# A four-layer graph network on one core: the opening and the job order of a pair are rearranged

## The chip, the core and the metric

One of the eight cores of a Trainium2 chip runs the kernel; the time is device microseconds of that core. TensorE (PE) multiplies matrices, VectorE (DVE), ScalarE (ACT) and GpSimd (POOL) do the elementwise work, and SyncE (SP) starts most transfers. Each engine takes its own instructions strictly in the order in which they were written.

## The reference, cut to what matters

`x` has shape (32, 512, 64): 32 batch items, 512 nodes, 64 features. `adj` is a 512 x 512 graph. Four layers each do `x = x + f(relu(layernorm(x)))`:

```python
# layer 0, three times:  v = relu([v, adj @ v] @ W1.T + b1) @ W2.T + b2
# layer 1, two times:    z = relu((adj @ z) @ w[i])
# layer 2, 8 heads and one output layer, each:
s = (h @ h.T) * graph;  s = where(s == 0, -1e16, s);  out = softmax(s) @ h + b
# layer 3:  e = leaky_relu(src[:, None] + dst[None, :]) * adj;  out = softmax(e) @ h + bias
```

Nearly all the work is in layer 2: per item, nine softmaxes over 512 x 512 scores.

## The kernel before, in words

**Tiling.** Two items make a pair, and 16 pairs go through the core. A pair's *front* (layers 0 and 1 and the features of layer 2; `front`, a generator of 25 steps F0 to F24) runs beside the attention of the pair before. F0 to F2 are a layernorm, F3 turns it, F4 to F12 are the three steps of layer 0 (in turn: a product with the weights at line 329, its copy to SBUF, and lines 363 and 317, which multiply with the turned graph `AT`, with the ReLU at line 366), F13 ends layer 0 (line 370 adds the residual), F14 to F16 are a layernorm, F17 to F20 layer 1, F21 to F23 a layernorm, F24 features.

**Units.** Attention is split into *units*, one softmax over 128 x 8 x 512 scores each: `a` to `d` and `g` to `j` are the eight head units of a pair (two heads of one item in each), `f` is the output layer of the pair before (`Out`), `e` the fourth layer of the pair before that (`Last`). For a unit:

- `s0`..`s3` make its scores: for a head or `f`, eight matmuls at line 427 and four at 430 that add the mask, into two of the four score buffers (`ps_s`, in PSUM); for `e`, two ScalarE instructions (line 699);
- `r0`..`r7` multiply by the graph and take row maxima on VectorE (line 448); each odd one also issues a negation on GpSimd (455);
- `x0`..`x3` are two exponentials each on ScalarE (459);
- `nA`, `nB` take reciprocals on VectorE (469), and normalise with four instructions each on GpSimd (471);
- `t0`..`t3` transpose 32 x 32 blocks on VectorE (477).

Two units share a weighted sum, `vA`..`vD` followed by the sum's number 0 to 4: 256 matmuls (line 487; 756 for sum 2, which weighs `e` and `f`). All four transposes of both units must be done before `vA`. For a pair of head units follow `us` (four ScalarE copies, 542), `w0 y0 w1 y1` (projections on PE at 521, four activations at 532), `o`, `c` (output product at 550, VectorE copy or add at 563 and 566), and for the second sum of an item `f0` or `f1` (571) and `h0` or `h1` (593, with 16 transfers on SP's queue). `k` and `Y` make the keys of the next two units (PE at 804, two ScalarE copies at 814). `eu`, `er`, `oA`..`oC`, `oT`, `oW`, `oN` follow sum 2: eviction, residual, a layernorm, and the features of the fourth layer (651, 662, with 36 transfers). `ZQ1` issues 16 transfers with the values of a pair's second item, which sums 3 and 4 read.

**Buffers that order the work.** All matmul results but the scores share four PSUM buffers (`ps_m`, tag `mm`), taken in turn: a sum holds four, `w0`, `w1` and `k` two each, `o` one. So `k` can begin only when the activations `y0` have read the two buffers that `w0` had. The softmax tiles (`sm`) are three, so a unit's first maximum waits until the sum that read the unit three before it has ended.

**What sets the order.** `manual_schedule` keeps the instructions in the order in which Python calls them. The jobs are called by tick (ten per pair) and, within a tick, by a rank, both from the dictionary `PLACES`, one (tick offset, rank) for each job name. It holds for every pair. What falls past the last tick follows the list `TAIL`, in which `T` and `U` are the last sums of the last pair, `E` its sum 2, `e` and `q` the fourth layer of pairs 13 and 14, `p` and `r` the output layer of pairs 14 and 15, `s` the fourth layer of pair 15.

**The opening.** Before the ticks the first pair's front runs alone, with the setup jobs of `among` between its steps (weights turned, graph turned, biases, masks `NEGM`, the four `factors` on A2, grams, vectors). Six steps of the second pair's front are called in it, after its steps 6 to 11 (`HEAD = 6`). Weights and biases are loaded by ScalarE's queue (lines 130 to 140), everything else by SP's.

Of the kernel before, what the change touches and what calls it, by code (L numbers as in the profile page):

```python
# [21 lines left out]
def gnn_stack_kernel(  # L22
# [107 lines left out]
    for j, r in enumerate(R):  # L130
        for k in range(2):
            nc.scalar.dma_start(out=W1n[r, k, r], in_=W1[:, k * D : (k + 1) * D])
        nc.scalar.dma_start(out=W2n[r, r], in_=W2)
    for k, b in enumerate((b1, b2, b_out, bias3)):
        for r in R:
            nc.scalar.dma_start(out=rows[H + k : H + k + 1, r], in_=b.rearrange("(o d) -> o d", o=1))
    nc.scalar.dma_start(out=rows[0:H, :], in_=bh)
    for j in range(2):
        nc.scalar.dma_start(out=ivt[:, j, :], in_=iv)
        nc.scalar.dma_start(out=b2bc[:, 0, j, :], in_=b2.partition_broadcast(P))  # L140
# [27 lines left out]
    I2b = const.tile([P, D], BF16, name="I2b")  # L168
# [13 lines left out]
    def graph_turned():  # L182
        for s in range(NT):
            pt = mm_ps()
            for t in range(NT):
                nc.tensor.transpose(pt[:, blk(t)], A[:, t, blk(s)], ident)
            nc.scalar.copy(AT[:, s, :], pt)
# [7 lines left out]
    def weights_joined():  # L195
        pt = mm_ps()
        for k in range(2):
            nc.tensor.matmul(pt[:, blk(k)], lhsT=W2n, rhs=W1T[:, k, 0, :], start=True, stop=True)
        nc.tensor.matmul(pt[:, 2 * P : 3 * P], lhsT=b2rep, rhs=W1T[:, 1, 0, :], start=True, stop=True)
        nc.tensor.matmul(pt[:, 3 * P : 3 * P + 1], lhsT=W1T[:, 0, 0, :], rhs=b2c, start=True, stop=True)  # L200
        for k in range(2):
            nc.vector.tensor_copy(W1T[:, k, 1, :], pt[:, blk(k)])
        nc.vector.tensor_copy(ubc[:, 0, :], pt[:, 2 * P : 3 * P])
        nc.vector.tensor_tensor(b1s, pt[:, 3 * P : 3 * P + 1], b1c, ALU.add)

    def masks():
# [3 lines left out]
        nc.vector.tensor_copy(I2b, II[:, 0, :])  # L210
# [21 lines left out]
    def grams():  # L232
# [5 lines left out]
        nc.vector.tensor_copy(WT.rearrange("p h d -> p (h d)"), pt)  # L238
# [4 lines left out]
        nc.vector.tensor_copy(G.rearrange("p h d -> p (h d)"), pt)  # L243
# [552 lines left out]
    def keys(ua, ub):  # L796
# [25 lines left out]
    HEAD = 6  # L822
    among = {
        0: [weights_turned],
        1: [biases, weights_joined, graph_turned],
        7: [masks],
        8: [lambda: factors(0)],
        9: [lambda: factors(1)],
        10: [lambda: factors(2)],
        11: [lambda: factors(3)],  # L830
        14: [grams],
        15: [vectors],
    }
    for n, _ in enumerate(first):
        for fn in among.get(n, ()):
            fn()
        if 6 <= n < 6 + HEAD:
            next(second)
# [3 lines left out]
        "begina": (0, 20), "s0a": (0, 21), "s1a": (0, 27), "s2a": (0, 97), "s3a": (0, 147), "r0a": (0, 81),  # L842
        "r1a": (0, 139), "r2a": (0, 148), "r3a": (0, 163), "r4a": (0, 214), "r5a": (0, 237),
        "r6a": (0, 242), "r7a": (0, 308), "x0a": (0, 253), "x1a": (0, 293), "x2a": (0, 298), "x3a": (1, 74),
        "t0a": (1, 118), "t1a": (1, 186), "t2a": (1, 285), "t3a": (1, 284), "nAa": (0, 310),
        "nBa": (1, 145), "beginb": (-1, 295), "s0b": (-1, 296), "s1b": (-1, 309), "s2b": (0, 195),
        "s3b": (0, 108), "r0b": (0, 52), "r1b": (0, 54), "r2b": (0, 57), "r3b": (0, 155), "r4b": (0, 234),
        "r5b": (0, 281), "r6b": (0, 226), "r7b": (0, 228), "x0b": (0, 88), "x1b": (0, 255), "x2b": (0, 314),
        "x3b": (0, 252), "t0b": (1, 84), "t1b": (1, 117), "t2b": (1, 102), "t3b": (1, 172), "nAb": (0, 286),
        "nBb": (1, 6), "beginc": (-1, 223), "s0c": (-1, 241), "s1c": (-1, 224), "s2c": (0, 166),  # L850
        "s3c": (0, 170), "r0c": (0, 83), "r1c": (0, 86), "r2c": (-1, 287), "r3c": (0, 37), "r4c": (0, 194),
        "r5c": (0, 248), "r6c": (0, 180), "r7c": (0, 185), "x0c": (0, 178), "x1c": (0, 174),
        "x2c": (0, 302), "x3c": (1, 33), "t0c": (0, 236), "t1c": (0, 299), "t2c": (1, 275), "t3c": (1, 268),
        "nAc": (0, 208), "nBc": (1, 49), "begind": (-1, 273), "s0d": (-1, 274), "s1d": (0, 28),
        "s2d": (0, 136), "s3d": (0, 71), "r0d": (0, 26), "r1d": (0, 46), "r2d": (0, 59), "r3d": (0, 78),
        "r4d": (0, 153), "r5d": (0, 182), "r6d": (0, 140), "r7d": (0, 203), "x0d": (0, 60), "x1d": (0, 163),
        "x2d": (0, 209), "x3d": (0, 238), "t0d": (0, 319), "t1d": (1, 0), "t2d": (1, 29), "t3d": (1, 38),
        "nAd": (0, 262), "nBd": (0, 294), "begine": (0, 41), "s0e": (0, 42), "s1e": (0, 62),
        "s2e": (0, 159), "s3e": (0, 55), "r0e": (0, 44), "r1e": (0, 132), "r2e": (0, 112), "r3e": (0, 152),
        "r4e": (0, 211), "r5e": (0, 216), "r6e": (0, 76), "r7e": (0, 161), "x0e": (0, 204), "x1e": (0, 183),  # L860
        "x2e": (1, 1), "x3e": (0, 258), "t0e": (1, 93), "t1e": (1, 162), "t2e": (1, 212), "t3e": (1, 263),
        "nAe": (0, 246), "nBe": (1, 129), "beginf": (-1, 103), "s0f": (-1, 312), "s1f": (-1, 104),
        "s2f": (0, 87), "s3f": (0, 151), "r0f": (0, 22), "r1f": (0, 77), "r2f": (-1, 239), "r3f": (-1, 261),
        "r4f": (0, 95), "r5f": (0, 179), "r6f": (0, 167), "r7f": (0, 259), "x0f": (0, 250), "x1f": (0, 173),
        "x2f": (0, 272), "x3f": (0, 290), "t0f": (0, 315), "t1f": (1, 43), "t2f": (1, 114), "t3f": (1, 122),
        "nAf": (0, 270), "nBf": (1, 9), "beging": (-1, 256), "s0g": (-1, 257), "s1g": (-1, 277),
        "s2g": (0, 68), "s3g": (0, 2), "r0g": (-1, 297), "r1g": (-1, 301), "r2g": (-1, 307), "r3g": (0, 23),
        "r4g": (0, 169), "r5g": (0, 229), "r6g": (0, 126), "r7g": (0, 142), "x0g": (0, 15), "x1g": (0, 47),
        "x2g": (0, 255), "x3g": (0, 249), "t0g": (0, 300), "t1g": (0, 311), "t2g": (1, 63), "t3g": (1, 64),
        "nAg": (0, 232), "nBg": (0, 260), "beginh": (0, 11), "s0h": (0, 12), "s1h": (0, 39), "s2h": (0, 99),  # L870
        "s3h": (0, 113), "r0h": (0, 75), "r1h": (0, 98), "r2h": (0, 105), "r3h": (0, 115), "r4h": (0, 124),
        "r5h": (0, 164), "r6h": (0, 133), "r7h": (0, 146), "x0h": (0, 100), "x1h": (0, 131),
        "x2h": (0, 215), "x3h": (0, 184), "t0h": (0, 265), "t1h": (1, 65), "t2h": (0, 288), "t3h": (0, 306),
        "nAh": (0, 192), "nBh": (0, 230), "begini": (0, 4), "s0i": (0, 5), "s1i": (0, 8), "s2i": (0, 67),
        "s3i": (0, 106), "r0i": (0, 13), "r1i": (0, 14), "r2i": (0, 16), "r3i": (0, 53), "r4i": (0, 111),
        "r5i": (0, 121), "r6i": (0, 190), "r7i": (0, 191), "x0i": (0, 80), "x1i": (0, 119), "x2i": (0, 235),
        "x3i": (1, 40), "t0i": (1, 89), "t1i": (1, 130), "t2i": (1, 243), "t3i": (1, 271), "nAi": (0, 267),
        "nBi": (1, 90), "beginj": (-1, 221), "s0j": (-1, 222), "s1j": (-1, 289), "s2j": (0, 144),
        "s3j": (0, 120), "r0j": (-1, 279), "r1j": (0, 17), "r2j": (0, 56), "r3j": (0, 61), "r4j": (0, 171),
        "r5j": (0, 254), "r6j": (0, 210), "r7j": (0, 225), "x0j": (0, 109), "x1j": (0, 220),  # L880
        "x2j": (0, 305), "x3j": (0, 280), "t0j": (0, 313), "t1j": (1, 66), "t2j": (1, 72), "t3j": (1, 176),
        "nAj": (0, 264), "nBj": (0, 318), "vA0": (1, 177), "vB0": (1, 198), "us0": (2, 25), "w00": (2, 70),
        "y00": (2, 82), "w10": (2, 127), "y10": (2, 150), "k0": (-1, 321), "Y0": (0, 10), "vA1": (1, 149),
        "vB1": (1, 156), "us1": (1, 282), "w01": (2, 32), "y01": (2, 45), "w11": (2, 134), "y11": (2, 143),
        "k1": (-1, 128), "Y1": (-1, 141), "vA2": (1, 135), "vB2": (1, 168), "vA3": (1, 137),
        "vB3": (1, 219), "us3": (2, 24), "w03": (2, 48), "y03": (2, 94), "w13": (2, 138), "y13": (2, 181),
        "k3": (-1, 187), "Y3": (-1, 189), "vA4": (1, 213), "vB4": (1, 233), "us4": (1, 304), "w04": (2, 34),
        "y04": (2, 85), "w14": (2, 116), "y14": (2, 125), "k4": (-1, 269), "Y4": (-1, 322), "o01": (2, 196),
        "c01": (2, 205), "o03": (2, 188), "c03": (3, 92), "f0": (4, 240), "h0": (5, 51), "o11": (2, 247),
# [160 lines left out]
```

## Time and profile before

| | us |
|---|---|
| three runs, median | 2334.38 (2334.08 to 2336.33) |
| the profiled execution, its own time | 2338.17 |
| its span | 2336.3 |
| first score block of the first pair (line 427) starts at | 82.88 |
| from one pair's line 370 to the next, pairs 8 to 9 | 135.5 |
| last pair's line 370 starts at | 2019.7 |

The page gives busy time by engine and by slice of the span. A row of the timeline is: start, length, engine, line, operation, tiles, count, and in brackets how long the engine had been idle and what released it. Matmul ends are modelled, so the length of a PE row runs over the start of the next one: prices of PE work are taken from start to start. A waits row is: who waited for whom, microseconds in all, times, the longest.

### The profile page before, as it was taken

To read this page: it belongs to the slowest core of one execution; us is meant where nothing else is said; L and a number is where in the kernel's file an instruction comes from. 1 tells how busy PE (TensorE), PEld (TensorE's weight loads), DVE (VectorE), ACT (ScalarE), POOL (GpSimd) and SP (SyncE) were. 2 spreads that over 40 slices of the span, in tenths; PEclk is the share of its full clock that TensorE was granted. 3 is DMA by queue.
4 is the path that set the end of the run, shared out by engine and by line. 5 is a ranking of instruction groups with operands and counts; after the bars stand their busy time and mean duration, and the time that the engine had idled before them with its cause. 6 is when DMAs were issued, how large, how long until landed. Compare 5 with 4: busy or idle time off the path is not lost.

```text
span 2336.3 us, 78517 instructions
## 1 busy us (share of the span) xinstructions
PE 2186.7 (94%) x32683; PEld 1172.3 (50%) x32683; DVE 1857.4 (80%) x4100; ACT 1493.1 (64%) x3752; POOL 1299.6 (56%) x2175
## 2 busy tenths in 40 slices
PE   6889999999999999999999999999999999999863
PEld 3435555555555555555555555555555555555342
DVE  3558788879888888988888898888888898887653
ACT  1346557667676766767676676767666676766544
POOL 2345465656666565565656466565656556655342
PEclk9899999999999999999999999999999999999886
DMA  5001111202121120212112021211202111211112
GB/s 122 11 15 21 25 20 23 42 14 39 21 41 26 24 42 13 41 21 39 25 27 40 13 42 21 37 25 29 39 15 42 20 31 25 31 32 19 22 25 46
DMA packets 279047, 70.20 MB, mean 30 GB/s; under 512 B 275100, under 2 KB 276132, under 8 KB 278692
## 3 DMA queue, kind: packets, MB, share of 16 engines
q1 hardware_dynamic: 277888, 65.02, 16.8%
q8 instruction: 256, 4.19, 0.8%
q14 instruction: 99, 0.81, 0.1%
q10 hardware_dynamic: 804, 0.17, 0.0%
HBM read 10.49 MB, written 4.19 MB: 6 GB/s over the span
## 4 chain that ended last, share of the span: by engine, by line
PE 76%; ACT 9%; DVE 6%; POOL 2%; SPq 2%; issue 1%; DMA 1%; ACTq 0%; DVEq 0%; POOLq 0%
PE s L427 20%; PE mm L487 17%; PE mm L317 9%; ACT sm L459 6%; PE mm L550 5%; PE mm L756 5%; PE mm L521 5%; PE s L430 5%; DVE sm L477 4%; PE mm L329 3%; PE mm L804 3%; SPq L299 2%; PE mm L363 1%; DVE sm L448 1%; PE mm L593 1%
## 5 line engine op out<-in xcount | busy, mean ns | idle before, releaser
L459 ACT ACTIVATE sm<-sm,nmx 128x512 f32<-128x512 f32 x1280 | 911.0, 720 | 238.5 <-POOL nmx L455 238.2
L471 POOL TENSOR_SCALAR sm<-sm,rs 128x512 f32<-128x512 f32 x1280 | 869.8, 699 | 149.1 <-DVE rs L469 109.0
L448 DVE CUSTOM_DVE_ANT_0 sm<-s,A 128x512 f32<-128x512 f32 x1152 | 734.0, 679 | 146.3 <-PE s L430 119.8
L477 DVE STREAM_TRANSPOSE sm<-sm 128x1024 f32<-128x1024 f32 x640 | 769.4, 1224 | 39.5 <-POOL sm L471 38.4
L427 PE MATMUL s<-ZZ,Y 64*64 64x512 f32 x4096 | 572.1, 605 | 24.9 <-ACT Y L814 14.0
L487 PE MATMUL mm<-sm,vq 32*64 32x256 f32 (+1 forms) x17152 | 502.7, 380 | 26.0 <-DVE sm L477 18.3
L455 POOL TENSOR_SCALAR nmx<-mx 128x2 f32<-128x2 f32 x640 | 148.3, 235 | 600.6 <-DVE mx L448 544.7
L487 PEld LDWEIGHTS mm<-sm,vq 32*64 32x64 f32 x17152 | 401.8, 135 | 141.7 <-issue 55.9
L427 PEld LDWEIGHTS s<-ZZ,Y 64*64 64x64 f32 x4096 | 146.9, 132 | 250.2 <-issue 112.9
L430 PE MATMUL s<-NEGM,I2b 64*64 64x512 bf16 x2304 | 257.9, 378 | 0.0
L459 ACT ACTIVATION_READ_ACCUMULATOR sm<-sm,nmx 128x1 f32 x1280 | 251.2, 196 | 0.0
L542 ACT COPY us<-mm 128x256 f32<-128x256 f32 x256 | 76.2, 382 | 156.6 <-PE mm L487 156.4
L317 PE MATMUL mm<-AT,v 128*128 128x512 f32 x384 | 173.6, 595 | 0.0
L532 ACT ACTIVATE y<-mm,cols 128x512 f32<-128x512 f32 x256 | 159.2, 684 | 11.1 <-PE mm L521 11.0
L268 POOL TENSOR_TENSOR xc<-x,nmu 128x512 f32<-128x512 f32 x48 | 54.8, 1141 | 192.1 <-DVE nmu L266 192.1
L430 PEld LDWEIGHTS <-I2b 64*64 64x64 bf16 x2304 | 81.0, 107 | 159.8 <-issue 159.2
L521 PE MATMUL mm<-us,Wh 64*64 64x512 f32 x1024 | 133.9, 592 | 23.1 <-ACT us L542 23.1
L277 POOL TENSOR_TENSOR r<-ve,mhalf 128x8 f32<-128x8 f32 x64 | 110.8, 1731 | 44.9 <-DVE ve L275 41.1
L756 PE MATMUL mm<-sm,vq 32*64 32x256 f32 x3712 | 118.0, 380 | 10.2 <-DVE sm L477 8.8
L550 PE MATMUL mm<-y,Wo_sb 128*64 128x512 f32 x512 | 126.9, 605 | 0.0
L317 PE MATMUL mm<-AT,z 128*128 128x512 f32 x256 | 120.1, 613 | 2.1 <-DVE z L281 1.4
L317 PEld LDWEIGHTS mm<-AT,v 128*128 128x128 f32 x384 | 73.2, 191 | 93.3 <-issue 91.7
(134 smaller groups left out, 2002.0 us busy)
## 6 DMA issues: line engine op xcount, KB each, us to landing
vq<-z SPq DMA_DIRECT2D x512, 32.0 KB, 1.9
vq<-hn SPq DMA_DIRECT2D x512, 32.0 KB, 1.9
vq<-h3n SPq DMA_DIRECT2D x512, 32.0 KB, 1.9
A<-in_adj_dram SPq DMA_DIRECT2D x5, 1024.0 KB
xt<-in_x_dram SPq DMA_DIRECT2D x32, 128.0 KB, 2.3
out_dram<-xo SPq DMA_DIRECT2D x32, 128.0 KB, 2.9
src<-src SPq DMA_DIRECT2D x64, 1.0 KB, 1.9
Wh<-in_L_gnn_Wh_dram SPq DMA_DIRECT2D x2, 256.0 KB
```

The costliest lines, as they stand in the source:

```text
L317: nc.tensor.matmul(pe, lhsT=v[:, m].rearrange("p j d -> p (j d)"), rhs=AT[:, m, :], start=(first and m == 0), stop=(m == NT - 1),)
L427: nc.tensor.matmul(pss[half][R[ab], :], lhsT=lhsT, rhs=rhs, start=True, stop=False)
L430: nc.tensor.matmul(pss[half][R[ab], :], lhsT=I2b[R[half], :], rhs=NEGM[R[half], k, :], start=False, stop=True,)
L448: nc.vector.tensor_tensor_reduce(self.sm[:, s, :], src, graph, 1.0, -FMAX, ALU.mult, ALU.max, self.mx[:, s : s + 1])
L459: nc.scalar.activation(self.sm[:, s, :], self.sm[:, s, :], AF.Exp, bias=self.nmx[:, s : s + 1], accum_out=self.ssum[:, s : s + 1],)
L471: nc.gpsimd.tensor_scalar(self.sm[:, s, :], self.sm[:, s, :], self.rs[:, s : s + 1], 1.0, ALU.mult, ALU.mult)
L477: nc.vector.transpose(out=two, in_=two)
L487: nc.tensor.matmul(self.u[i][R[c], 0 : weights.shape[1] * 32], lhsT=values[32 * i : 32 * i + 32, jb, :], rhs=weights[32 * i : 32 * i + 32, ...
L521: nc.tensor.matmul(py[c][r, :], lhsT=Wh2[R[c], 2 * (self.q - 1 + c) + ab, r], rhs=self.us[R[c], 2 * ab : 2 * ab + 2].rearrange("p i (s e) ...
L532: nc.scalar.activation(y, py[c], AF.Prelu, bias=cols[:, h : h + 1], alpha=0.01)
L550: nc.tensor.matmul(pa[R[ab], :], lhsT=Wo_sb[:, h, :], rhs=self.y[h], start=(k == 0), stop=(k == 1),)
L756: nc.tensor.matmul(self.u[i][r, 0 : N // 2], lhsT=values[i // 2][q, jb, :], rhs=sm[q, :, 32 * jb : 32 * jb + 32], start=(jb == 0), stop=(j ...
```

## The change: what it does

1. **Opening.** `W1` is loaded with two transfers in place of four. `ivt` is loaded ahead of the biases. The 64 x 64 identity `I2b` is made by two ScalarE copies between ScalarE's own transfers, no longer by VectorE in `masks`. The graph is turned right after the weights, ahead of the biases, and two of its four PSUM copies go to VectorE. The joined weights and joined biases become two jobs. The grams' two copies go to ScalarE. `masks` comes two steps later, `factors` eight steps later (after the first pair's steps 16 to 19).
2. **Second pair's front.** Twelve of its steps are called in the opening, not six: after steps 6 to 11 as before, and six more (F6 to F11) beside the first pair's two later layernorms, after steps 14 to 16 and 21 to 23.
3. **Jobs.** Every entry of `PLACES` is new, and `TAIL` is a new list. No instruction of a pair is added or taken away.

```diff
-    for j, r in enumerate(R):
-        for k in range(2):
-            nc.scalar.dma_start(out=W1n[r, k, r], in_=W1[:, k * D : (k + 1) * D])
+    for r in R:
+        nc.scalar.dma_start(out=W1n[r, :, r], in_=W1.rearrange("o (k d) -> o k d", k=2))
         nc.scalar.dma_start(out=W2n[r, r], in_=W2)
+    for j in range(2):
+        nc.scalar.dma_start(out=ivt[:, j, :], in_=iv)
+    I2b = const.tile([P, D], BF16, name="I2b")
+    for r in R:
+        nc.scalar.copy(I2b[r], ident[r, r])
...
-            nc.scalar.copy(AT[:, s, :], pt)
+            (nc.scalar.copy, nc.vector.tensor_copy)[s % 2](AT[:, s, :], pt)
...
+    def biases_joined():
+        pt = mm_ps()
+        nc.tensor.matmul(pt[:, 0:P], lhsT=b2rep, rhs=W1T[:, 1, 0, :], start=True, stop=True)
+        nc.tensor.matmul(pt[:, P : P + 1], lhsT=W1T[:, 0, 0, :], rhs=b2c, start=True, stop=True)
+        nc.vector.tensor_copy(ubc[:, 0, :], pt[:, 0:P])
+        nc.vector.tensor_tensor(b1s, pt[:, P : P + 1], b1c, ALU.add)
...
-    HEAD = 6
+    BESIDE = (6, 7, 8, 9, 10, 11, 14, 15, 16, 21, 22, 23)
+    HEAD = len(BESIDE)
     among = {
         0: [weights_turned],
-        1: [biases, weights_joined, graph_turned],
-        7: [masks],
-        8: [lambda: factors(0)],
-        9: [lambda: factors(1)],
-        10: [lambda: factors(2)],
-        11: [lambda: factors(3)],
+        1: [graph_turned],
+        2: [weights_joined],
+        3: [biases],
+        5: [biases_joined],
+        9: [masks],
         14: [grams],
-        15: [vectors],
+        16: [lambda: factors(0)],
+        17: [lambda: factors(1), vectors],
+        18: [lambda: factors(2)],
+        19: [lambda: factors(3)],
     }
...
-        if 6 <= n < 6 + HEAD:
+        if n in BESIDE:
             next(second)
```

Sorted by tick and rank, the new `PLACES` give nearly the old order on every engine in a middle pair. These are the places that differ and matter:

```
PE, sum 4:        old  vA vB vC vD s0b s1b w0          new  vA vB s0b vC vD s1b w0
PE, after it:     old  w0 s3b w1 k1 s2b o13            new  w0 s3b s2b w1 k1 o13
PE, oW:           old  after o01, ahead of oN          new  between F9 and f1, half a pair earlier
PE, after sum 1:  old  s0f w0 s2f w1 s3f k3 o03        new  s0f s2f w0 w1 s3f k3 o03
ACT, after sum 1: old  us x2e y0 y1 x1f Y3             new  us x2e x1f y0 y1 Y3
PE, after k4:     old  s0i s1i h0 s2i s3i              new  h0 s0i s1i s2i s3i
DVE, unit d:      old  r6d r4d r5d r7d c01 nAd t3c t2c nBd src t0d
                  new  r6d t2c r7d r4d r5d nAd t3c t0d src nBd c01
DVE, unit e:      old  t3d r0e F13 r6e F14 r2e r1e r3e F15 r7e r4e r5e F16 r2f nAe r3f r0f r1f t0e r4f nBe
                  new  t3d F13 r0e F14 r1e r2e r4e r3e F15 r6e r7e r5e F16 r2f r3f nAe r0f r1f r4f nBe t0e
SP:               old  ZQ1 in tick 5, behind oN's 36   new  ZQ1 in tick 1, ahead of h1's 16
```

In the last pair, whose ticks hold no front, the same places apply; `TAIL` differs most in the maxima of units `r` (pair 15's output layer), of which two stand behind the transposes that end sum `E`, where all eight stood ahead of them.

## The prediction

> **What bounds the kernel now.** I read the page's busy shares and slices first, then the waits of PE, then timelines of one middle pair, of the opening and of the last pair.
>
> ```profile
> span 2336.3 us, 78517 instructions
> PE 2186.7 (94%) x32683; PEld 1172.3 (50%) x32683; DVE 1857.4 (80%) x4100; ACT 1493.1 (64%) x3752; POOL 1299.6 (56%) x2175
> PE   6889999999999999999999999999999999999863
> PEclk9899999999999999999999999999999999999886
> ```
>
> PE is idle for 2336.3 − 2186.7 = 149.6 us. By the slices (58.4 us each) that lies at both ends. Summing PE's gaps in the trace gives about 33 us before 100 us, 72 after 2085, and 2.5 in each middle pair (135.5 from one line 370 to the next, PE busy 132.9, DVE 115.6). So PE sets the middle, and nothing can shorten a middle pair by much: PE's instructions stay the same. The opening and the end have slack. The waits of PE:
>
> ```profile
> PE mm L521 <- ACT us L542: 23.1, 14, 1.7
> PE s L427 <- ACT Y L814: 14.0, 17, 2.8
> PE mm L401 <- POOL z L290: 8.1, 1, 8.1
> PE mm L487 <- DMA vq<-z: 2.4, 2, 1.9
> ```
>
> The first two are the only gaps of a middle pair (1.70 and about 0.7). The third is in the opening, the fourth in the last pair. The timeline around the first, after sum 1 of a middle pair:
>
> ```profile
> 1082.17 1.15 ACT L542 COPY us<-mm 128x256 f32<-128x256 f32 x4
> 1082.84 1.09 PE L521 MATMUL mm<-us,Wh 64*64 64x512 f32 x8 [1.70 <-ACT us L542]
> 1084.63 2.53 ACT L532 ACTIVATE y<-mm,cols 128x512 f32<-128x512 f32 x4
> 1086.76 1.04 PE L804 MATMUL mm<-ZZ,G 64*64 64x256 f32 x16
> ```
>
> In the opening the windows view shows PE waiting and then paying for it with its clock (columns: window, length, busy time of each engine, granted clock, DMA share, GB/s):
>
> ```profile
> 42.00:46.00 4.00, 2.34 (x46) 2.01 (x45) 2.14 (x4) 0.00 (x0) 1.57 (x2) 1.00 0.41 89
> 46.00:50.00 4.00, 0.95 (x4) 0.59 (x3) 2.83 (x8) 0.00 (x0) 2.15 (x2) 0.50 0.00 0
> 50.00:57.00 7.00, 6.70 (x8) 2.52 (x8) 0.00 (x0) 0.13 (x1) 0.00 (x0) 0.56 0.00 0
> 59.00:63.10 4.10, 3.70 (x8) 1.44 (x8) 0.00 (x0) 0.30 (x1) 0.00 (x0) 1.00 0.00 0
> 70.00:80.00 10.00, 6.32 (x24) 3.01 (x25) 0.69 (x1) 1.66 (x3) 2.16 (x2) 0.50 0.19 32
> ```
>
> The same aggregation (line 317, eight matmuls) takes 6.70 us at clock 0.56 and 3.70 at 1.00. The last pair's sum 3:
>
> ```profile
> 2173.78 10.24 SPq L299 DMA_DIRECT2D vq<-z  x16
> 2180.98 0.61 PE L487 MATMUL mm<-sm,vq 32*64 32x256 f32 x2 [0.46 <-DMA vq<-z]
> 2183.53 6.64 PE L487 MATMUL mm<-sm,vq 32*64 32x256 f32 x122 [1.93 <-DMA vq<-z]
> 2195.08 0.69 DVE L448 CUSTOM_DVE_ANT_0 sm<-s,A 128x512 f32<-128x512 f32 x1 [12.21 <-PE mm L487]
> ```
>
> Its values arrive late, behind the 36 transfers of oN, and DVE then stands for 12.21 us, since the first maximum of unit `j` needs a buffer that sum 3 frees.
>
> **1, the opening.** I walked the new order with durations of before.
> - Weights turned ahead: same transfers, nothing. Graph turned ahead, two copies on VectorE: the first pair's step-0 aggregation starts at 19.7, not 22.2, because fewer PE and ScalarE jobs stand ahead of it: −2.5.
> - The four factors (1.2 us each on VectorE) move from steps 8–11 to 16–19. Line 230 held VectorE 2.98 us for A2's transfer, and PE then had a 1.45 stall at 33.74. Third step's projection is ready at 38.9, not 42.55, and the layernorm's `z` at 46.3, not 50.0: −3.7 so far.
> - Beside that layernorm PE now has F6 (1.0 + 3.6), a 0.7 turn's wait and F7 (1.17), ahead of the aggregation: it starts at 47.9, 1.6 later than `z` allows, but with PE busy, at 3.6 instead of 6.70. It ends 51.5, not 56.84.
> - The vectors move to step 17 (0.8 between its products): residual ready 60.8, not 65.67.
> - F9 and F10 beside the third layernorm (1.0 + 3.6 + 0.7 + 1.17 = 6.5) hide in its 7.4 us; uncovered they would cost at most 6.5. Line 401 starts at 68.1, not 73.01. From there the throttled stretch falls away (line 804 1.98 to about 1.1, and lines 363 and 317, 2.07 + 4.37, no longer stand ahead of the scores): the first score block starts at about 71.5, not 82.88: **−11.4**.
> - From there to sum 0 of the first pair (107.82 before) VectorE's maxima and transposes set the pace. F8 and F11 (0.69 each) have left it: another −1.5 to −2.
>
> Sum **−13**. Ends: −17.7 if idle of VectorE before sum 0 shrinks as well, and −8 if transfers of `A` and `W1` land as late as before and VectorE, given two more graph copies, pushes the layernorms.
>
> [...]
>
> **2, a middle pair.** PE's order from sum 3 to the last scores of unit `d` (1126.1 to 1196.4) has no gap; there only added PE time counts, and time that leaves.
> - `oW` (0.96 at its rows) moves in between F9 and `f1`: +0.96 here, less after sum 2.
> - Sum 4 is cut by `s0b` and `s1b` in two places instead of behind it: sum and blocks take 9.29 before; the 256 matmuls cut as 3.64 + 3.64 with the block between (1.24 where both neighbours have the other tiling, 1.08 otherwise) come to 9.64: +0.35. Together +1.3.
>
> The rest (1196.4 to the next 1126.1, 65.2 us) is set by VectorE's chain to the transposes before sums 2 and 3, with PE waiting at `us` and `Y`.
> - VectorE waits 1.23 there before `t2d` (row at 1196.51). `t2c` moves into that wait, of which a transpose's 1.17 would fill 0.7: −0.7.
> - ScalarE after sum 1: `x1f` (0.72 × 2 = 1.4) goes ahead of `y0`. Line 542's copies to the first `y` stays 1.8; the four activations end at 1087.2 before, 1088.6 now. `w1` waits for nothing of `y0` now and stands ahead, but `k3` needs `y0`'s two PSUM buffers, so PE waits about 1.4 there instead of 1.70 at `w0`, which `s2f` (1.1) now covers. Queued behind `k3` on PE: `o03`, `s0g`; each 0.5 to 1.0 later against sum 1. `nBe` also waits for the later `x2e`, 0.5 ahead of `t0e`. VectorE has work until the maxima of `g`, so I pass 0.1 through.
> - `h0` (16 PE, 16 transfers on SP) ahead of `s0i`: SP has nothing due then; 0. `ZQ1` ahead of `h1`: `h1`'s transfers start 16 issues later (16 x 0.64, the spacing of SP's issues in the last ticks: 10 us), needed half a pair on; 0.
>
> Sum +1.3 − 0.7 + 0.1 = **+0.7 a pair**. Ends: −0.3, if `s2f` and `s3b` cover what PE waits for now (1.70 + 0.7) and only half the 1.3 shows; +1.6, if the 1.0 at `s0g` passes through. Over 13.5 pairs **+9**, from −4 to +22.
>
> [...]
>
> **3, the last pair.** `ZQ1` in tick 1 is ahead of oN's 36 transfers: sum 3's first half took 10.2 us (2179.88 to about 2190) against 3.64 where its values are in: −6.6, and the 12.21 of VectorE shrinks with it. Two maxima of unit `r` (0.69 each) leave the way to sum `E`, whose wait for transposes was 8.80: −1.2. From `E` on SP's issues of 2 × 36 transfers set the end, 62.2 us from the attention sources to the end of the span: unchanged. **−7**; −12 if other units of `TAIL` move forward with it, +3 if the missing cover of the last ticks (no front) makes the cut sum 4 wait.
>
> **The sum.** −13 + 9 − 7 = −11. The profiled execution took 2338.17 (span 2336.3 and 1.9 around it), 3.8 above the median; 2338.2 − 11 = 2327.2 in its terms, **2323.4** against the median of 2334.38.
>
> **Rivals.**
> - *A: as worked out* (chance 0.5), 2315 to 2331.
> - *B: the other side, slower.* `x1f` ahead of `y0` delays `k3`, `o03` and `s0g`, and it isn't hidden: each pair's maxima of unit `g` and all behind them come 1.0 later on top of the 1.3. +2.3 × 13.5 = +31, −20 at both ends: 2345. It decides from +1.5 a pair on (20 / 13.5). For it: PE has 2.5 us of slack in a pair and VectorE 20, but not at every place. Against: VectorE has maxima of other units there. 0.2.
> - *C: the new order closes the gaps of PE.* Both waits go (1.70 + 0.7), less the 0.6 of a switch-heavy sum 4: −1.8 a pair, −24, with −20 at the ends: 2290. The floor is PE's 132.9 a pair. 0.1.
> - *D: it does nothing.* The opening gives half (−6), since VectorE sets it all the way, the last pair gives nothing because the freed sum 3 runs into the next wait, and +0.4 a pair takes 5: 2334. 0.2.
>
> **How the numbers follow.** A difference under 0.2% (4.7 us: 2329.7 to 2339.1) can't be told from none. Of A, 0.42 is faster and 0.08 within the bound; B gives 0.19 slower and 0.01 within; C 0.1 faster; D 0.05 faster, 0.13 within, 0.02 slower. Faster 0.57, same 0.22, slower 0.21. The range reaches from 2306 (opening −17.7, end −12, a pair at 0) to 2343 (a pair at +2.1 with both ends as reckoned), which leaves C's lower half and B's upper half out.
>
> **What would show it.** Right: clock 1.00 from 20 us on, line 317's aggregation of `z` at about 48 taking 3.6, first scores at about 71.5; the wait for `us` at the projections under 1 us and a new one of about 1.4 at the keys (line 804, now 808) for `y`; a period near 136.2; sum 3 of the last pair in about 8.5 us with no wait for `vq`. Wrong: a clock of 0.5 in the opening; a period over 137 or under 135; VectorE waiting for score blocks of `g`; sum `E` no earlier against the last line 370.

## The result, and the profile after

| | before | changed |
|---|---|---|
| median of 12 runs | 2334.36 us | 2338.10 us |
| all runs | 2332.32 to 2336.33 | 2335.51 to 2341.25 |
| profiled execution, its own time | 2338.17 | 2335.51 |
| first score block starts (line 427 / 431) | 82.88 | 76.17 |
| second pair's line 370 / 374 | 131.31 | 125.76 |
| fourth such line | 395.4 | 389.7 |
| median from one to the next, middle pairs | 135.29 | 136.31 |
| from the last one to the end of the span | 316.6 | 307.9 |

The changed kernel is slower by a factor of 1.0018 (95% interval 1.0010 to 1.0027), +4.2 us of 2334.4. That is just inside the 0.2% which the prediction called no difference, and not the 11 us forecast as a gain. The two profiled executions alone differ the other way, by -2.7; that of before stood 3.8 above its median, that of the change 2.6 below. So the terms below are taken from the rows, and their sum is tested with timed runs.

Line numbers of the changed kernel are those of before plus 3 for lines 169 to 198, and plus 4 for lines 211 to 821. The page of the changed kernel:

```profile
span 2333.6 us, 78508 instructions
PE 2202.7 (94%) x32683; PEld 1174.1 (50%) x32683; DVE 1854.0 (79%) x4099; ACT 1503.3 (64%) x3754; POOL 1298.6 (56%) x2175
PE   7889999999999999999999999999999999999863
PEclk9999999999999999999999999999999999999996
```

PE is busier by 16 us with the same 32683 matmuls. Its waits (who waited for whom, us, times, longest):

```profile
PE s L431 <- DVE mx L452: 33.3, 35, 6.3
PE mm L808 <- ACT ZZ L407: 3.7, 16, 0.7
PE s L431 <- ACT Y L818: 3.5, 3, 2.2
PE mm L525 <- ACT us L546: 1.6, 2, 0.8
```

The two waits of a middle pair before (23.1 for `us`, 14.0 for `Y`) are nearly gone, and a wait of score blocks for VectorE's maxima stands there instead. Its place is the stage after sum 1, in the timeline:

```profile
1081.08 0.68 DVE L452 CUSTOM_DVE_ANT_0 sm<-s,A 128x512 f32<-128x512 f32 x1
...
1081.83 1.35 PE L431 MATMUL s<-HH 64*64 64x512 f32 x6 [1.34 <-DVE mx L452]
...
1082.10 1.17 ACT L546 COPY us<-mm 128x256 f32<-128x256 f32 x4
...
1085.97 2.41 ACT L536 ACTIVATE y<-mm,cols 128x512 f32<-128x512 f32 x4
...
1086.71 1.66 PE L808 MATMUL mm<-ZZ,G 64*64 64x256 f32 x16
```

The maximum of 1081.08 is `r2f`. `s2f` needs the score buffer that it frees, so PE stands 1.34 ahead of `s2f` where it stood 1.70 ahead of `w0`. The keys (line 808) begin at 1086.71 and run on only as `y` frees their buffers: 1.59 to the next line's start, 0.97 before.

In the opening, windows (length, busy time and count of PE, its weight loads, VectorE, ScalarE, GpSimd; then granted clock, DMA share, GB/s):

```profile
9.00:16.00 7.00, 4.74 (x21) 3.64 (x21) 2.41 (x5) 1.06 (x5) 1.11 (x1) 1.00 0.49 140
16.00:23.00 7.00, 6.31 (x22) 4.88 (x23) 1.95 (x8) 1.70 (x4) 0.00 (x0) 0.51 1.09 216
42.00:46.00 4.00, 3.33 (x44) 2.95 (x44) 1.55 (x3) 0.91 (x2) 1.79 (x2) 0.69 0.29 66
50.00:57.00 7.00, 5.66 (x21) 2.69 (x19) 3.25 (x6) 1.27 (x2) 0.00 (x0) 1.00 0.00 0
70.00:80.00 10.00, 6.83 (x47) 2.72 (x49) 2.60 (x6) 1.66 (x3) 1.66 (x2) 0.71 0.23 36
```

The aggregation of `z` (50 to 57) has its full clock, as forecast. But the trace has PE at half clock from 16.2 to 23.0, from 43.5 to 46.9, from 74.2 to 81.1, where the first scores start, and from 101.5 to 105.0: 20.5 us. In before it is from 46.0 to 56.2 and from 66.5 to 80.1: 23.9 us. The clock of 1.00 in the row of 9 to 16 is no measurement up to 12.8: the trace's record of the clock starts there, at 1.00 (in before at 18.7). The rows show a slower PE ahead of it, in the turning of the graph:

```profile
10.27 3.36 PE L189 MATMUL mm<-ident,A 128*128 128x128 f32 x16
```

Up to 12.6 these transposes start 0.21 us apart, at the end of the row 0.11, as such transposes (lines 313 and 405) do in a middle pair. In before all but the last three start 0.21 apart.

And sum 3 of the last pair, with the start of sum E:

```profile
2186.30 3.71 PE L491 MATMUL mm<-sm,vq 32*64 32x256 f32 x128
...
2191.17 3.71 PE L491 MATMUL mm<-sm,vq 32*64 32x256 f32 x128
...
2243.80 2.82 PE L760 MATMUL mm<-sm,vq 32*64 32x256 f32 x42 [2.98 <-DVE sm L481]
```

Sum 3 takes 8.51 (2186.30 to the next block at 2194.81) with no wait for its values; sum E starts 218.0 after the last line 374, 227.9 before.

### The profile page after: what moved, and what is told of

Read it like the earlier page. It is cut to its first block, busy times and chain, and to the rows that moved or that the text cites. A ratio compares the mean times of both kernels' runs of the same rounds, so it can differ in the third digit from the quotient of the medians.

```text
span 2333.6 us, 78508 instructions
## 1 busy us (share of the span) xinstructions
PE 2202.7 (94%) x32683; PEld 1174.1 (50%) x32683; DVE 1854.0 (79%) x4099; ACT 1503.3 (64%) x3754; POOL 1298.6 (56%) x2175
## 4 chain that ended last, share of the span: by engine, by line
PE 53%; DVE 18%; ACT 12%; POOL 9%; issue 3%; SPq 2%; DMA 1%; DVEq 0%; ACTq 0%; POOLq 0%
PE s L431 14%; PE mm L491 12%; ACT sm L463 9%; PE mm L321 7%; DVE sm L452 7%; DVE sm L481 7%; POOL sm L475 5%; PE mm L554 4%; PE s L434 3%; PE mm L525 3%; PE mm L808 2%; SPq L303 2%; PE mm L333 2%; ACT y L536 1%; PE mm L367 1%
## 5 line engine op out<-in xcount | busy, mean ns | idle before, releaser
L431 PE MATMUL s<-ZZ,Y 64*64 64x512 f32 x4096 | 580.0, 609 | 20.0 <-DVE mx L452 13.7
L491 PE MATMUL mm<-sm,vq 32*64 32x256 f32 (+1 forms) x17152 | 495.6, 378 | 28.7 <-issue 11.0
L491 PEld LDWEIGHTS mm<-sm,vq 32*64 32x64 f32 x17152 | 392.2, 134 | 149.0 <-issue 74.8
L434 PE MATMUL s<-NEGM,I2b 64*64 64x512 bf16 x2304 | 269.3, 378 | 0.0
L525 PE MATMUL mm<-us,Wh 64*64 64x512 f32 x1024 | 140.0, 589 | 1.6 <-ACT us L546 1.6
L473 DVE RECIPROCAL rs<-ssum 128x4 f32<-128x4 f32 x320 | 53.9, 168 | 89.7 <-ACT sm L463 89.4
```

What stands on the lines that cost most here:

```text
L431: nc.tensor.matmul(pss[half][R[ab], :], lhsT=lhsT, rhs=rhs, start=True, stop=False)
L434: nc.tensor.matmul(pss[half][R[ab], :], lhsT=I2b[R[half], :], rhs=NEGM[R[half], k, :], start=False, stop=True,)
L491: nc.tensor.matmul(self.u[i][R[c], 0 : weights.shape[1] * 32], lhsT=values[32 * i : 32 * i + 32, jb, :], rhs=weights[32 * i : 32 * i + 32, ...
L525: nc.tensor.matmul(py[c][r, :], lhsT=Wh2[R[c], 2 * (self.q - 1 + c) + ab, r], rhs=self.us[R[c], 2 * ab : 2 * ab + 2].rearrange("p i (s e) ...
```

## The experiments

All ratios are to before, timed in the same series (its medians were 2333.9 to 2335.9), with 95% intervals. A stretch is the time from one sum's start to the next, the median of nine middle pairs; the sums follow each other as 1, 2, 3, 4, 0. The column "pair" is the median of ten middle pairs, from one line 370 (or 374) to the next, so it need not be the sum of the stretches (in `e5_sum1` the pairs run from 136.85 to 138.39).

| kernel | pair | 1 to 2 | 2 to 3 | 3 to 4 | 4 to 0 | 0 to 1 |
|---|---|---|---|---|---|---|
| before | 135.29 | 26.64 | 26.95 | 29.32 | 27.73 | 24.64 |
| changed | 136.31 | 27.51 | 26.54 | 29.59 | 28.89 | 23.78 |
| `e4_early_r2f` | 138.90 | 29.76 | 26.92 | 29.60 | 28.89 | 23.78 |
| `e5_sum1` | 137.71 | 28.89 | 26.91 | 29.58 | 28.89 | 23.78 |
| `e6_uncut` | 135.98 | 27.52 | 26.54 | 29.58 | 28.54 | 23.78 |
| `e11_ow` | 137.52 | 27.23 | 26.53 | 29.58 | 27.87 | 26.29 |
| `f4_x1f` | 135.72 | 26.85 | 26.93 | 29.61 | 28.55 | 23.78 |
| `e12_s2f` | 135.11 | 26.45 | 26.95 | 29.32 | 27.73 | 24.64 |

### Halves: the jobs alone, the opening alone

`e1_jobs` is before with the new dictionary and list:

```diff
-        "begina": (0, 20), "s0a": (0, 21), "s1a": (0, 27), "s2a": (0, 97), "s3a": (0, 147), "r0a": (0, 81),
+        "begina": (0, 9), "s0a": (0, 10), "s1a": (0, 19), "s2a": (0, 104), "s3a": (0, 117), "r0a": (0, 81),
...
-        e:begine e:s0e 7:t2j 7:t3j 7:nBj e:r0e p:beginf p:s0f e:s1e e:r2e e:s2e T:vA4 e:r3e e:r1e e:x1e T:vB4
+        e:begine e:s0e e:s3e 7:t2j e:s1e e:s2e 7:t3j p:beginf p:s0f T:vA4 T:vB4 e:r0e e:r1e T:vC4 e:r2e e:r3e
...
```

> The opening of before with the new PLACES and TAIL. The two profiled executions give +11.8 us for the middle pairs (136.3 against 135.3 a pair) and -8.7 for the end, so theory A (the profiles speak for all executions) says +3 against before, 2337.5. Theory B says that the 6.4 us by which the medians (+3.7) and the profiles (-2.7) disagree come from the jobs, which would then cost +9.4 with the opening giving -5.7: 2344. Theory C puts the 6.4 into the opening, which then gives nothing: +3 to +4 here. The period should be 136.3 in each case, which confirms that no part of it comes from the opening.

Measured 2343.29, ratio 1.0035 (1.0021 to 1.0049), +8.2; period 136.35. `e2_opening` is the changed kernel with this edit the other way round, the old dictionary and list in place of the new.

> The new opening (twelve steps of the second pair in it) with the old PLACES and TAIL. Theories A and B: -5.7, 2328.7, with the period of before, 135.3. Theory C (the opening of before is not always as slow as in its profile, with its two stretches at half clock, or the new one not always as fast): 0 to -1, 2333.5 to 2334.4. In its trace the first score block starts near 76, not 82.9, and the first aggregation at about 23, not before 22.2, as in the changed kernel.

Measured 2329.77, 0.9979 (0.9970 to 0.9988), -4.9; period 135.31. The parts add: +8.2 - 4.9 = +3.3 against +4.2 measured. Theory B holds: the opening wins 5, the jobs lose 8. The scores began at 76.78, the first aggregation at 23.82.

### The middle pairs

`e4_early_r2f`: changed, with

```diff
-        "r2f": (0, 11), "r3f": (0, 17),
+        "r2f": (-1, 248), "r3f": (-1, 249),
```

> The changed kernel with r2f and r3f, the maxima that free the score buffers for s2f, called three maxima earlier on VectorE (behind F15, ahead of r6e, r7e, r5e). Theory M: after sum 1 PE's wait for us (1.70 a pair) was only replaced by s2f's wait for r2f (1.34 and about 0.5 behind it), because s2f now stands ahead of w0; with r2f and r3f early the wait goes, the period falls from 136.3 to 134.6 to 135.0, and the time by 18 to 23 us to 2315 to 2320. Rival: the gapless PE time (134.2 a pair) has grown by itself, by cutting sum 4 and by more changes of tiling, and another wait (us, or the transposes of unit e, whose maxima come 1.4 later) takes the place: period 136.0 to 136.4, no change from 2338.

Measured 2368.78, 1.0146 (1.0132 to 1.0160): much slower, neither theory's number. The timeline:

```profile
1092.71 0.69 DVE L452 CUSTOM_DVE_ANT_0 sm<-s,A 128x512 f32<-128x512 f32 x1 [1.03 <-PE mm L491]
...
1097.38 1.17 ACT L546 COPY us<-mm 128x256 f32<-128x256 f32 x4
...
1098.05 1.95 PE L525 MATMUL mm<-us,Wh 64*64 64x512 f32 x16 [2.60 <-ACT us L546]
```

`r2f` is the first maximum of unit `f`: its softmax tile is one that sum 1 is still reading. Called early it blocks VectorE for 1.03 until the sum ends, and behind it stand three maxima of unit `e`, their exponentials on ScalarE, and behind those `us`. So `r2f` cannot come much earlier, and `us` stands behind unit `e`.

`e5_sum1`: changed, with the stage after sum 1 in its old order:

```diff
-        "s2f": (0, 28), "x1f": (0, 31),
+        "s2f": (0, 30), "x1f": (0, 226),
```

> The changed kernel with the stage after sum 1 in its old order: s2f behind w0 again (PE), x1f behind both y again (ScalarE). Theory S (the pair grew by 1.0 because here s2f's wait for r2f, 1.34, and the keys' wait for the later y0 took the place of the 1.70 for us): the stretch from sum 1 to sum 2 falls from 27.6 back to 26.6, the period from 136.3 to 135.3 to 135.5, the time by 10 to 13 us to 2325 to 2328. Rival G (the gapless stretch from sum 3 to unit d's scores grew by 1.45, from oW and the cut sum 4, and this sets the period): the period stays within 0.2 of 136.3, since what is won after sum 1 is lost again at the transposes before sum 2.

Measured 2352.42, 1.0085 (1.0071 to 1.0098). Neither: the stretch grew by another 1.4, with PE's wait for `us` back and larger than ever:

```profile
PE mm L525 <- ACT us L546: 30.8, 15, 2.7
```

The two moves of this stage, taken together, are thus no cause of the loss; in the new surroundings they hold it down. `f4_x1f` below parts them.

`e6_uncut`: changed, sum 4 in one piece.

```diff
-        "beginb": (-1, 250), "s0b": (-1, 251),
+        "beginb": (-1, 250), "s0b": (-1, 278),
```

> The changed kernel with s0b called behind vD4, so that sum 4 is in one piece of 256 matmuls again. Theory G: this stretch is gapless on PE, so the 0.35 that the cut costs in the trace (9.64 against 9.29 from the sum's start to w0) comes back whole: period 135.95, time -4.5 us, 2333.6. Theory S: the 0.35 goes into waits further on (s2b, the keys), period 136.2 to 136.3, time within 1.5 us of 2338.

Measured 2333.83, 1.0004 (0.9995 to 1.0013), 3.3 us below the changed kernel's ratio. The period fell by 0.33, all of it in the stretch from 4 to 0 (28.89 to 28.54). The cut's 0.35 is paid in full.

`e11_ow`: this with `oW` also back.

```diff
-        "oW": (7, 166),
+        "oW": (8, 255),
```

> The changed kernel with sum 4 in one piece (period 135.98 as measured) and oW in its old place, between o01 and oN. Theory G, as predicted: the pair is a series of a gapless stretch of PE (sum 3 to unit d's scores), which sheds 0.96, and a chain of waits behind it (d's maxima, exponentials, oN, its transfer, unit e, us), which gains up to 0.57, the copy of oW that then stands ahead of oN's on ScalarE: period 135.0 to 135.6, time -5 to -13 against 2333.8, 2321 to 2329. Rival: the chain takes all of it, period 136.0.

Measured 2352.52, 1.0075 (1.0062 to 1.0087). The stretch from 4 to 0 shed 0.67, as it should; the next grew by 2.51:

```profile
PE mm L367 <- ACT h3T L657: 18.0, 13, 1.4
```

`oW`'s copy now stands behind the exponentials of unit `d`, and F12's product on PE (line 367) waits 1.4 a pair for the PSUM buffer that this copy reads; unit `e`'s first score product and all that follows stand behind it on PE. Moving `oW` was neither the cost of the change nor free to undo.

`f4_x1f`: `e6_uncut` with ScalarE's half of the stage put back.

```diff
-        "x1f": (0, 31),
+        "x1f": (0, 226),
```

> The changed kernel with sum 4 in one piece (2333.8, period 135.98), and of the stage after sum 1 ScalarE's order alone put back: x1f behind both y, while s2f stays ahead of w0. My rival B of the prediction (x1f ahead of y0 makes the keys and all behind them 1.0 later) expects the stretch from sum 1 to sum 2 to fall from 27.5 to 26.5 to 26.9 and the period to 135.0 to 135.4; time -8 to -13. The other reading: VectorE's transposes of e and f wait for x1f through f's normalisation, which then comes later, and nothing is won or up to 0.5 a pair lost: period 136.0 to 136.5.

Measured 2331.27, 0.9985 (0.9977 to 0.9994). The stretch from 1 to 2 falls by 0.67, as rival B said; 0.39 of it comes back from 2 to 3, and the pair gains 0.26. `x1f` ahead of `y0` does cost, a quarter of what rival B charged.

### The opening

`e7_i2b`: changed, `I2b` made by VectorE as before.

```diff
-        nc.scalar.copy(I2b[r], ident[r, r])
...
+        nc.vector.tensor_copy(I2b, II[:, 0, :])
```

> The changed kernel with I2b made by VectorE in the masks, as before, and no longer by ScalarE between its transfers. Theory Q: ScalarE's copies of the turned W1 start at 14.9 in the changed kernel, behind its own issues of transfers, against 13.8 before, because the two copies into I2b wait for the identity and push those issues back; PE's wait then also halves its clock (the first products at lines 333 and 367 take 2.08 and 2.05, not 1.16 and 1.02). Without them the copies start near 13.8, the first aggregation at about 21 to 22 rather than 22.9 to 23.8, the first scores 2 us earlier, the time -1.5 to -3 us: 2335 to 2336.6. Rival: ScalarE's issues are held up by the transfers themselves, and the copies come at 14.5 or later in any case: no change, 2338.

Measured 2340.18, 1.0026 (1.0017 to 1.0034); no gain.

```profile
13.17 0.43 ACT L180 COPY W1T<-mm 128x128 f32<-128x128 f32 x2
14.98 0.69 DVE L188 COPY AT<-mm 128x512 f32<-128x512 f32 x1 [3.02 <-PE mm L187]
15.59 0.68 DVE L284 SCALAR_TENSOR_TENSOR z<-xc,r 128x512 f32<-128x512 f32 x1
16.45 0.27 DVE L200 COPY W1T<-mm 128x128 f32<-128x128 f32 x1
19.10 1.23 PE L332 MATMUL mm<-W1T,zT 128*128 128x128 f32 x4 [0.47 <-ACT zT L314]
```

ScalarE's copies did come 1.8 earlier (13.17, 14.94 in the changed kernel). But the copy of the joined weights stands on VectorE behind a graph copy and `z`, and the first product (line 332 here) came at 19.10, 18.52 in the changed kernel.

`e10_graph`: changed, the graph turned behind the joined weights.

```diff
-        1: [graph_turned],
-        2: [weights_joined],
+        2: [weights_joined, graph_turned],
```

> The changed kernel with the graph turned behind the joined weights again, as before, the two copies still on VectorE. Theory H: with the graph turned ahead, PE has little to do between 14 and 18 us, its clock falls to half, and the first step's products and part of its aggregation pay for it (2.08, 2.05 and 4.1 to 4.7 us, where they took 1.16, 1.02 and 3.7 before); in the old place the transposes stand just ahead of them and keep the clock up: the first aggregation starts at 21 to 22 instead of 23 to 23.8, and the first scores and the whole time come 1.5 to 2.5 us earlier, 2335.6 to 2336.6. Rival: the transposes then delay the first step by what they take (3.3), as the change must have meant to avoid: first aggregation at 23 or later, no gain or 1 us lost.

Measured 2340.36, 1.0020 (1.0011 to 1.0029). The first products did take their short time (line 333 1.16, as at 51.61 in the changed kernel, at a clock of 1.00), but the first aggregation started at 24.88: the rival's case. The transposes ahead of them did not run at full clock themselves, as Theory H had it: from 17.66 to 21.07 they started 0.21 apart. With the graph turned early line 333 starts 4.1 sooner (18.52, here 22.58) and the aggregation 1.9 (22.95): about half of what the order wins is lost by then, most of it at lines 333 and 367 (2.08 and 2.05 at a clock of 0.50, here 1.16 and 1.10).

`e9_beside9`: changed, no steps beside the second layernorm.

```diff
-    BESIDE = (6, 7, 8, 9, 10, 11, 14, 15, 16, 21, 22, 23)
+    BESIDE = (6, 7, 8, 9, 10, 11, 21, 22, 23)
```

> The changed kernel with nine steps of the second pair in the opening: none beside the second layernorm, so that F9 to F11 fall to the job order, as F6 to F11 did before. Theory P (the prediction's own term was too small here: F6 and F7 ahead of the aggregation of z put it 2.9 us later than z allows, 52.6 against 49.7): the aggregation starts at about 49.7, and even at half clock (6.4) ends near 56, as in the changed kernel; the first scores come 4 to 6 us later than its 76.2, because the products of a step at lines 367 and 321 then stand ahead of them again, and the time is +3 to +5, 2341 to 2343. Theory K (the clock is what matters): the aggregation takes 6.4 to 6.7 again, the chain loses 3 more: first scores at 84, 2345.

Measured 2339.48, 1.0016 (1.0007 to 1.0025), the changed kernel's own ratio: both theories wrong. The first scores came at 74.91, and these three steps are worth nothing.

`f1_order` is the reordering alone, `e2_opening` with

```diff
-    BESIDE = (6, 7, 8, 9, 10, 11, 14, 15, 16, 21, 22, 23)
+    BESIDE = (6, 7, 8, 9, 10, 11)
```

> The old job order, the new order of the setup jobs, and only the six old steps of the second pair in the opening: the reordering alone. Theory R (the steps won, the reordering lost): the first aggregation comes at 23 or later as in all kernels with this order (22.6 to 23.8, against 21.3 to 22.3 with the old one), and with the old six steps the first scores come 0 to 2 us later than the old 80.7 to 82.9; time 0 to +2 against before, 2335 to 2337. Rival (the prediction's step): the factors moved out of the way win 3.7 here, 2331.

Measured 2333.95, 0.9997 (0.9989 to 1.0006). First aggregation 23.13, first scores 81.62.

`f2_steps` is before with the twelve steps and nothing else.

```diff
-    HEAD = 6
+    BESIDE = (6, 7, 8, 9, 10, 11, 14, 15, 16, 21, 22, 23)
+    HEAD = len(BESIDE)
...
-        if 6 <= n < 6 + HEAD:
+        if n in BESIDE:
```

> Before, with twelve steps of the second pair in the opening in place of six, and nothing else: the steps alone. Theory R: the first scores come 6 us earlier, near 75, since a product and aggregation (2.07 + 4.4 in the profile of before, lines 363 and 317) no longer stand ahead of them, the time falls by 5 to 7 us, 2328 to 2330, as much as the whole new opening (-5.2) or more. Rival: the six steps cost beside the layernorms what they save ahead of the scores (the kernel with nine steps was as fast as that with twelve): -2 to 0.

Measured 2336.42, 1.0008 (0.9999 to 1.0016). First scores 78.51, but the second pair's residual at 130.99, as late as in before:

```profile
75.00:80.00 5.00, 3.64 (x25) 1.30 (x28) 0.00 (x0) 1.66 (x3) 0.00 (x0) 0.50 0.30 49
100.00:110.00 10.00, 7.80 (x118) 3.91 (x122) 8.44 (x17) 2.93 (x8) 6.22 (x12) 0.72 0.01 2
```

What the steps won ahead of the scores was lost by that residual; PE ran sum 0 there at a clock of 0.72 (100 to 110). Neither part wins alone, together they win 4.9. That only the two together pay is measured; why is not settled.

`f3_warm`: changed, with eight transposes more in PE's wait at 13.6.

```diff
-        for s in range(NT):
+        for s in (0, 1, 3, 2):
...
-            for t in range(NT):
+            for t in list(range(NT)) * (3 if s == 2 else 1):
```

> The changed kernel with eight transposes more in the graph's last block (done three times over, the same values written), between 13.6 and 15.3 us, where PE otherwise waits for ScalarE's copies of W1: work that only keeps PE busy. Theory H: the clock then stays at 1.00 from 16 to 23 us, where it is 0.50 in the changed kernel; lines 333 and 367 take 1.16 and 1.02 again, the first aggregation comes at about 21, 2 us earlier, and the time falls by 1.5 to 2: 2336. Rival: the clock falls all the same, since PE still waits in pieces until 18.5; no change in the first aggregation (22.6 to 23.8), 2338.

Median 2337.02 of 12, 1.0011 (1.0002 to 1.0020); but the profiled execution took 2327.91, the eleven others 2333.82 to 2339.81. Its windows:

```profile
9.00:16.00 7.00, 5.98 (x29) 4.85 (x28) 2.49 (x5) 1.21 (x5) 1.00 (x1) 1.00 0.51 130
16.00:23.00 7.00, 6.41 (x29) 3.98 (x29) 1.87 (x7) 1.55 (x3) 0.00 (x0) 1.00 1.09 221
70.00:80.00 10.00, 8.64 (x92) 3.55 (x91) 5.51 (x18) 5.86 (x15) 1.01 (x5) 1.00 0.31 49
```

The clock reads 1.00 in every window from 16 to 95, with line 333 in 1.16, and 0.66 from 95 to 100: first aggregation at 19.95, first scores at 72.79, the second pair's residual at 120.10, 5.7 ahead of the changed kernel's. The filler does not bring this about reliably: in `g2_warm` below, with the same transposes, line 333 took 1.92 and not 1.16.

### The end, and what is faster than both

`e3_zq1` is before with one job moved, and `e8_open_zq1` is `e2_opening` with the same edit:

```diff
-        "ZQ1": (5, 36),
+        "ZQ1": (1, 166),
```

> Before, with ZQ1 alone moved from tick 5 (behind oN's 36 transfers) to tick 1, ahead of h1. Mechanism as predicted: the last pair's sum 3 takes 8.5 instead of 15 us, and 6.2 of the -8.7 at the end come from this: 2328, period unchanged at 135.3. Rival: the freed time runs into the next wait (VectorE's transposes before sum 4 and sum E, or SP's issues), and the gain is 0 to 2 us: 2332.4 to 2334.4, since in the changed kernel the new TAIL came with it.

Measured 2331.44, 0.9985 (0.9976 to 0.9994), -3.5; period 135.30, the end 312.6. About half the forecast 6.2 passed.

> The new opening with the old job order, and ZQ1 in tick 1: the two parts that won time, without the part that lost it. If the parts add, -5.2 and -3.5 against before: 2326.3, with the period at 135.3. If the first pair's tick 1 or SP's queue couples them, less: 2328 to 2330.

Measured 2326.12, 0.9970 (0.9959 to 0.9982), -7.0: the parts add as far as the intervals tell.

`e12_s2f` is this with `s2f` ahead of `w0`:

```diff
-        "s2f": (0, 87),
+        "s2f": (0, 31),
```

> The fastest kernel so far (new opening, old jobs, ZQ1 early, 2326.1, period 135.3) with s2f alone ahead of w0 after sum 1, as the change has it. In that order r2f has ended when s2f starts, so s2f fills the 1.70 in which PE waits for us: PE gets to the keys up to 0.9 earlier. If PE's place there sets the pair, the period falls to 134.4 to 134.8 and the time by 7 to 12 us, to 2314 to 2319. If VectorE's transposes before sum 2 set it (they end at the moment that sum 2 starts), the period falls by 0 to 0.2 and the time stays at 2323 to 2326.

Measured 2323.23, 0.9950 (0.9938 to 0.9963). The period fell by 0.2, the case expected if VectorE's transposes set it, not PE's place. It is the lowest median of the study, 11.7 us under before.

`g1_tail` is this with the new `TAIL` (the list's half of the edit of `e1_jobs`), `g2_warm` is this with the edit of `f3_warm`:

> The fastest kernel so far (2323.2: new opening, old jobs, ZQ1 early, s2f ahead of w0) with the new TAIL. In the profiles the end (from the last pair's line 370 or 374 on) lasts 305.9 to 313.2 us with the new TAIL and places, and 310.5 to 312.6 with ZQ1 alone early. If the rest of the end's gain (3 us on average) is the list's, 2320; if it comes from the places of the last pair's jobs, or is scatter, 2322 to 2325.

> The same kernel with the old TAIL and with the eight transposes more that keep PE busy in the opening. In the changed kernel they gave one execution at full clock throughout the opening (2327.9) and eleven others at 2333.8 to 2339.8. If the clock's part is worth 2 us in most executions, 2321; if the gate falls as often at another place, 2322.5 to 2324.

Measured 2326.23, 0.9955 (0.9942 to 0.9969), its end 310.3 against 310.5; and 2325.66, 0.9955 (0.9943 to 0.9967). Neither can be told from `e12_s2f`. The new list of the end adds nothing to an early `ZQ1` there.

## Why the prediction was wrong, by its own steps

Its sum was -13 + 9 - 7 = -11. In the runs it is about -4.9, +13.5 and -6.2, together +2.4, measured +4.2 (2.3 to 6.3).

- **The opening, -13: the step that failed**, by 8 of the 15 us. The walk itself was sound at full clock, as far as the first scores: "starts at 19.7" was 19.95 and "71.5" was 72.79 in the one execution of `f3_warm` whose clock reads 1.00 from 16 to 95. What failed was the sentence that "the throttled stretch falls away", and that the first aggregation comes 2.5 earlier: in the thirteen profiles with the graph early and no filler it starts at 22.6 to 24.0 (21.3 to 22.6 in the four with the old order), and in all thirteen the product ahead of it (line 333) takes 2.07 to 2.08, where it takes 1.16 in the four, in `e10_graph` and in `f3_warm`. The half clock did not fall away but moved: 10.2 and 13.7 us at two places before, 6.8, 3.4, 6.8 and 3.4 at four places now. F7 ahead of the aggregation of `z` cost more than the 1.6 reckoned: `z` is done at 49.66, the aggregation starts at 52.61.

  The last term, "another -1.5 to -2" up to sum 0, held only for the first eight matmuls of the sum: they start at 98.67 and not 107.82, 2.4 more than the first scores had won. Then PE waits for VectorE's transposes, and most of the rest begins at half clock (0.50 from 101.5 to 105.0):

```profile
101.98 8.57 PE L491 MATMUL mm<-sm,vq 32*64 32x256 f32 x248 [2.65 <-DVE sm L481]
```

  The block behind the sum starts at 110.48, 5.1 earlier than before (115.55), and the second pair's residual is 5.6 earlier: of 9.2 us won, 3.6 are gone there. With twelve steps of the second pair the clock is 0.83 from 100 to 110 us in the changed kernel, 0.72 in `f2_steps`, 0.84 in `e12_s2f` and 0.66 in `g2_warm`, and 0.66 from 95 to 100 in `f3_warm`; with six it is 1.00 from 95 to 110 in before, `f1_order`, `e1_jobs` and `e3_zq1`. These are profiles of one execution a kernel. How much of the timed 8 us each place takes stays open: the filler of `f3_warm` did not move its median clear of the changed kernel's.
- **A middle pair, +0.7.** The mechanism was right, the size too small: +1.02, 0.98 as a mean over twelve pairs. The gapless stretch (sum 3 to sum 0) grew by 0.27 + 1.16 = 1.43, forecast 1.3; the rest changed by -0.86 + 0.87 - 0.42 = -0.41, forecast -0.6. Of its terms the cut of sum 4 is shown (0.35 in the rows, 0.33 in `e6_uncut`). "The wait for `us` is covered by `s2f`" was half true: `s2f` waits itself, for `r2f`, because VectorE gets its tile only when sum 1 ends. The wait "of about 1.4 at the keys" for `y` came as 0.6 (1.59 against 0.97). The 1.23 that VectorE waits at 1196.51 stands, by the row, ahead of maxima (line 448) and not of `t2d`. Over 13.5 pairs the difference is 4 us.
- **The last pair, -7.** Right: the end lasted 315.8 on average in the four profiles with the old places and `ZQ1` late, 309.6 in the eleven with the new ones, -6.2. Sum 3 took the 8.5 forecast. `ZQ1` alone gave -4.5 of it (311.3 in four profiles), -3.5 in the timed run. The -1.2 charged to two maxima of unit `r` is not shown: in `g1_tail` the new list alone won nothing. What gave the rest stays open; the ends of the eleven scatter from 305.9 to 313.2.
- **The rivals.** B (slower, 2345) had the right place: `x1f` ahead of `y0` costs 0.67 after sum 1. But 0.39 comes back by sum 3, and its +1.5 a pair was never reached. D (nothing gained, 2334) lies nearest to the result, though not by its sum: it halved the opening rightly and set the last pair to nothing wrongly. C's gapless order did not come: one wait went and another stood in its place; and its 0.6 for sum 4 was an estimate that no run shows, the cut cost 0.35. The low end of the range adds up to 2304.7 (-17.7 and -12 from 2334.4), not 2306, which changes nothing here.
- **The clock and the tiling.** That F6 and F7 would keep the clock up ahead of the aggregation of `z` was the author's estimate, made although the row of 42 to 46 had warned (PE busy for 2.34 of 4 us, and 0.50 right behind it). In the changed kernel the clock fell to half at 43.5 us although PE had been busy for 2.04 of the 3.41 us before; it was back at 1.00 from 46.9, and the aggregation at 52.61 did take 3.60. The twelve executions of `f3_warm` spread from 2327.91 to 2339.81, and line 333 took 1.16 in its profile and 1.92 in that of `g2_warm`, with the same filler; what parts them is not shown. For the changes of tiling in sum 4 the price in the rows held: the cut cost its 0.35 and no more.

## What to carry to other kernels

Before an idle stretch of PE is counted as won, ask at what clock the work that moves there will run: here the rearrangements of the opening moved the half clock to other places (it began at 16.2 and 43.5 us after PE had been busy for 1.32 and 2.04 of 3.41), and a walk that added durations at full clock was right, up to the first scores, only for the one execution that had it. In a pair that is a ring of waits, a wait removed on one engine comes back as the next one in the ring, here the score buffer behind the tile behind the sum; undoing one move of a jointly arranged order can cost more than the whole order did. Parts that touch different stages (opening, end, one job's rank) do add, and taking only those that won gave 2323 where the whole change gave 2338.

## What the runs showed of the hardware

- The granted clock fell after stretches in which PE was only partly idle: in the changed kernel at 16.2 us after PE had been busy for 1.32 of 3.41 us, and at 43.5 after 2.04 of 3.41. In the traces of before and of the changed kernel every recorded stretch of half or full clock, but the last, lasts 3.41 us or a whole multiple of it. In these two, in the 3.41 us ahead of a fall PE was busy for at most 2.06 (its ends modelled), ahead of a rise for at least 2.97. Busy time does not settle it alone: in the changed kernel the clock stayed at 1.00 through 2251.93 to 2255.34 and beyond, with PE busy for 1.43 of it.
- The first transposes of the graph start 0.21 us apart in the changed kernel from 10.3 to 12.6 us, and 0.11 from 13.1. In `e10_graph`, with PE idle from 11 to 15, they still start 0.21 apart from 17.66 to 21.07.
- The clock column can miss it: where the trace has no record of the clock (up to 12.8 us in the changed kernel, 18.7 in before) it shows 1.00. For 16 to 23 us of `e11_ow` it shows 1.00 too, though line 333 took 2.08 there, as it did at a recorded 0.50 in the changed kernel. Row durations are the better witness.
- A profiled execution can stand 4 us above its kernel's median (before) or 9 below (`f3_warm`). The profile of `f3_warm` has a span 7.5 us shorter than that of the changed kernel with the same middle pairs (136.30 and 136.31): 5.7 of it lie before the second pair's residual and 2.0 after the last line 374. Where the other executions differ was not profiled.
